# One-pass values and sums, a cap by minimum and a new weave in the second layer of a two-layer AdaLN block

## The chip, the cores and the metric

The kernel runs on one core of one Trainium2 chip. Its five engines are TensorE (PE in the profile; PEld is its weight load), VectorE (DVE), ScalarE (ACT), GpSimd (POOL) and SyncE (SP, which here only issues DMAs). The metric is the device time of one execution in microseconds (us), as a median of several runs.

## The reference, cut to what matters

Eight sequences of 256 tokens with 512 channels go through two layers. Each layer has an attention-like part and a feed-forward part; each part is normed, scaled and shifted by vectors that come from a condition, and added to the residual. Layer 0 (a selective scan and a gated feed-forward part) is not touched by the change. Layer 1 is:

```python
h = _layernorm(x) * (1 + ca) + sa
q, k, v = (proj(wq), proj(wk), proj(wv))      # 32 heads of 16 channels
q, k = _apply_rope(q, sin, cos), _apply_rope(k, sin, cos)
scores = einsum('bnth,bnsh->bnts', q, k) / sqrt(16)
scores = where(causal, scores, -inf)
attn = softmax(scores)
x = x + ga * (einsum('bnts,bnsh->bnth', attn, v) @ wo.T)
h = _layernorm(x) * (1 + cb) + sb
x1, x2 = split(h @ w12.T + b12)
x = x + gb * ((silu(x1) * x2) @ w3.T + b3)
```

## The kernel before

**Layout.** Channels lie on the 128 partitions in four groups (index j or k, `NC` = 4), tokens on the free axis. All matmuls of layer 1 are in float32, except those that write the causal mask, which are in bfloat16. A float32 matmul of the program is two instructions in the profile.

**Heads.** A group of 128 channels holds eight heads of 16. Four strips of 32 rows (r) hold two heads each, the even and the odd one (e). `ke[e]` and `qe[e]` are copies of the rotated keys and queries in which the other head's rows are blanked by `em_sb` (1 for the rows of one parity, 0 for the other). In a blanked row `ke` carries a one, and into the same row of `qe` a DMA later puts minus the row's maximum, so that the second score matmul gives score minus maximum by itself.

**The work of one batch** is written as Python generators. Each `yield` ends a step.

- `before_scores(b)`, 8 steps: mean; variance and norm (`norm_steps`, lines 72 to 95); two groups of k, two of q (line 541, each with `rotary`, line 518); two of v (line 561), copied into a padded tile `vpad` (line 566).
- `maxima(b)`, 7 steps: six tiles of scores by query (`sc`, line 588, on top of a mask matmul, line 579), each reduced to its row maximum on VectorE (line 593); in the seventh the maxima are turned by a matmul (`pnt`, line 600), copied by ScalarE (`nmt`, line 605) and sent by eight DMAs from SP's queue into rows of `qe` (line 609).
- `weigh(b)`: six tiles of scores by key (`st`, line 629), again on top of a mask matmul (line 620), each followed by one exp on ScalarE (`pt`, line 634). Key block 1 is done for two channel groups at a time, key block 0 for one. `average(j)` (line 640) multiplies the weights with the values and, in a second pass with a matrix of ones (`sumw`), with ones: `av[:, 0]` holds the sums of values, `av[:, 1]` the sums of weights. VectorE takes the reciprocal (line 655) and multiplies (line 656).
- `after_average(b)`, 10 steps: output projection `po` (2 steps, line 676), mean and variance of the second norm, four groups of the feed-forward part `pf` (line 696) with Silu on ScalarE and one multiply on VectorE, two groups of `pw` (line 710), whose result ScalarE scales (`g`, line 716) and GpSimd adds to x (line 720).

**PSUM.** The score tiles `sc` and `st` fill four banks and there is one buffer of them (`ps_sc`), so the next tile's matmuls wait until ScalarE or VectorE has read the one before. `av` has one buffer (`ps_av`), the dense groups two (`ps_mm`), the statistics one (`ps_st`).

**Order.** TensorE's order in layer 1 is written by hand: `woven` runs the 14 steps of `scores(b)` and takes, behind each, the next step of `after_average(b - 1)` (stream 0) or of `before_scores(b + 1)` (stream 1) by the list `behind` in line 738. On the other engines a scheduler sets the order when the program is built; each of them then works its queue strictly in that order. While batch b's scores are made, the output part of batch b - 1 and the q, k and v of batch b + 1 thus fill in.

Of the kernel before, what the change touches and what calls it, by code (L numbers as in the profile page):

```python
# [18 lines left out]
P = 128  # L19
# [22 lines left out]
    return ap.unsqueeze(1).to_broadcast([ap.shape[0], n, ap.shape[1]])  # L42


@with_exitstack
def block(
    ctx: ExitStack, tc: tile.TileContext,
# [21 lines left out]
    xT = [None] * NB  # L69
    mod = [[const.tile([P, NC, NB], F32, name=f"mod{l}_{v}") for v in range(6)] for l in range(2)]  # L70

    def norm_steps(lnp, ps_st, b, shift, scale1, name, put):
        xb = xT[b]
        mean = ps_st.tile([P, L], F32, name=f"mean{name}", tag="st")
        for k in range(NC):
            nc.tensor.matmul(mean, ones, xb[:, k, :], start=(k == 0), stop=(k == NC - 1))
        xc = lnp.tile([P, NC, L], F32, name=f"xc{name}", tag="xc")
        nc.vector.tensor_tensor(xc, xb, bc(mean, NC), ALU.subtract)
        h = lnp.tile([P, NC, L], F32, name=f"h{name}", tag="h")
        sq = h  # L80
        nc.scalar.activation(sq, xc, AF.Square)
        yield
        var = ps_st.tile([P, L], F32, name=f"var{name}", tag="st")
        for k in range(NC):
            nc.tensor.matmul(var, ones, sq[:, k, :], start=(k == 0), stop=(k == NC - 1))
        rstd = lnp.tile([P, L], F32, name=f"rstd{name}", tag="rstd")
        nc.scalar.activation(rstd, var, AF.Ln, bias=eps)
        nc.scalar.activation(rstd, rstd, AF.Exp, scale=-0.5)
        nc.vector.tensor_tensor(xc, xc, bc(rstd, NC), ALU.mult)  # L89
        for k in range(NC):  # L90
            nc.gpsimd.tensor_scalar(  # L91
                h[:, k, :], xc[:, k, :], scale1[:, k, b : b + 1], shift[:, k, b : b + 1],
                ALU.mult, ALU.add,
            )
        put.append(h)

    ENG = mybir.EngineType
# [380 lines left out]
    w12_sb = load(attw, w12, "w12")  # L478
    b12_sb = load(attw, b12, "b12")
    w3_sb = load(attw, w3, "w3")  # L480
    b3_sb = load(attw, b3, "b3")
    gb3 = attw.tile([P, NC, NB], F32, name="gb3")
    nc.vector.tensor_tensor(
# [2 lines left out]
    identh = attw.tile([P, P], BF16, name="identh")  # L486
    nc.vector.tensor_copy(identh, ident)

    masks = []
    for name, sign in (("qk", 1), ("kq", -1)):  # L490
        m = attw.tile([P, P], BF16, name=f"mask{name}")
        nc.gpsimd.memset(m, 0.0)
        nc.gpsimd.affine_select(
            out=m, in_=m, compare_op=ALU.is_ge, fill=MASKED,
            base=0, pattern=[[-sign, P]], channel_multiplier=sign,
        )
        masks.append(m)
    mask_qk, mask_kq = masks
    swap = [(i // HD) * HD + (i % HD + HD // 2) % HD for i in range(32)]

    strips = attw.tile([P, 2, 4], F32, name="strips")
# [5 lines left out]
    one_row = attw.tile([P, 2], F32, name="one_row")  # L507
    nc.vector.tensor_reduce(one_row, strips, AX.X, ALU.add)

    sumw = attw.tile([P, 2, 2 * HD], F32, name="sumw")  # L510
    vps = [attw.tile([P, 2, NH // 2, 4, HD], F32, name=f"vpad{i}") for i in range(2)]
    nc.gpsimd.memset(vps[0], 0.0)
    nc.gpsimd.memset(vps[1], 0.0)
    nc.gpsimd.memset(sumw, 0.0)
    for e in range(2):
        nc.gpsimd.memset(sumw[:, e, e * HD : (e + 1) * HD], 1.0)

    def rotary(ps, dst, name):
        raw = att.tile([P, 2, L], F32, name=f"raw{name}", tag="raw")
        nc.scalar.copy(raw, ps)  # L520
        sw = att.tile([P, 2, L], F32, name=f"sw{name}", tag="sw", bufs=1)
        nc.vector.stream_shuffle(sw, raw, swap)
        nc.gpsimd.tensor_tensor(raw, raw, bc(rope_sb[:, 0, :], 2), ALU.mult)  # L523
        nc.vector.tensor_tensor(sw, sw, bc(rope_sb[:, 1, :], 2), ALU.mult)
        nc.gpsimd.tensor_tensor(dst, raw, sw, ALU.add)  # L525
# [3 lines left out]
    def before_scores(b):  # L529
# [6 lines left out]
        for w, isq in ((wk_sb, False), (wq_sb, True)):  # L536
            for k0 in range(0, NC, 2):
# [10 lines left out]
                for e in range(2):  # L548
                    if isq:
                        nc.scalar.activation(qe[e][:, cols, :], rot, AF.Copy, scale=em_sb[:, e : e + 1])  # L550
                    else:
# [2 lines left out]
                            scale=em_sb[:, e : e + 1], bias=one_row[:, e : e + 1],  # L554
                        )
                yield
        vp = vps[b % 2]
        for t in range(2):
            pv = ps_mm.tile([P, NH // 2, 2, HD], F32, name=f"pv{b}_{t}", tag="mm")
# [5 lines left out]
            for e in range(2):  # L565
                nc.vector.tensor_copy(vp[:, t, :, 3 * e, :], pv[:, :, e, :])
            yield
        qs[b], ks[b] = qe, ke

    def maxima(b):  # L570
        qe, ke = qs[b], ks[b]
# [40 lines left out]
    def weigh(b):  # L612
        qe, ke, vp = qs.pop(b), ks.pop(b), vps[b % 2]
        pts = {}

        def weights(kb, js):
            Q = L - kb * P
            sc = ps_sc.tile([P, 4, len(js), 2, Q], F32, name=f"st{b}_{kb}_{js[0]}", tag="sc")
            for r in range(4):
                nc.tensor.matmul(  # L620
                    sc[:, r, :, :, :P], identh,
                    mask_kq.unsqueeze(1).unsqueeze(1).to_broadcast([P, len(js), 2, P]),
                    start=True, stop=False, skip_group_check=True,
                )
            for j in js:
                for e in range(2):
                    for r in range(4):
                        rows = slice(32 * r, 32 * r + 32)
                        nc.tensor.matmul(  # L629
                            sc[:, r, j - js[0], e, :], ke[e][rows, j, kb * P : (kb + 1) * P],  # L630
                            qe[e][rows, j, kb * P :], start=False, stop=True, skip_group_check=True,
                        )
            pt = att.tile([P, 4, len(js), 2, Q], F32, name=f"pt{b}_{kb}_{js[0]}", tag=f"pt{kb}", bufs=2 - kb)
            nc.scalar.activation(pt, sc, AF.Exp, scale=ATT_SCALE)  # L634
            for j in js:
                pts[kb, j] = pt[:, :, j - js[0]]

        ao = aos[b] = att.tile([P, NC, L], F32, name=f"ao{b}", tag="ao", bufs=1)

        def average(j):  # L640
            av = ps_av.tile([P, 2, L], F32, name=f"av{b}_{j}", tag="av")
            for kb in range(2):
                for e in range(2):
                    for what in range(2):
                        for r in range(4):
                            w = sumw[:, e, :]
                            if what == 0:
                                w = vp[:, kb, 4 * j + r, 2 * e : 2 * e + 2, :].rearrange("p a d -> p (a d)")
                            nc.tensor.matmul(  # L649
                                av[32 * r : 32 * r + 32, what, kb * P :], w, pts[kb, j][:, r, e, :],  # L650
                                start=(kb == 0 and e == 0 and what == 0), stop=(kb == 1 and e == 1),
                                skip_group_check=True,
                            )
            rec = att.tile([P, L], F32, name=f"rec{b}_{j}", tag="rec")
            nc.vector.reciprocal(rec, av[:, 1, :])  # L655
            nc.vector.tensor_tensor(ao[:, j, :], av[:, 0, :], rec, ALU.mult)

        for j in range(0, NC, 2):
            weights(1, (j, j + 1))
            yield  # L660
            weights(0, (j,))
            yield
            weights(0, (j + 1,))
            average(j)
            yield
            average(j + 1)
            if j + 2 == NC:
                yield

    def after_average(b):  # L670
        ao = aos.pop(b)
# [12 lines left out]
                )  # L684
            yield
        put = []
        yield from norm_steps(lnp, ps_st, b, mod[1][3], mod[1][4], f"d{b}", put)
        h = put[0]
        yield
        x4 = att.tile([P, NC, L], F32, name=f"x4_{b}", tag="x4", bufs=1)  # L690
        for i in range(M2 // P):
# [6 lines left out]
                        start=(k == 0), stop=(k == NC - 1),  # L698
                    )
            sl = att.tile([P, L], F32, name=f"sl{b}_{i}", tag="sl")  # L700
            nc.scalar.activation(sl, pf[:, 0, :], AF.Silu, bias=b12_sb[:, i : i + 1])  # L701
            nc.vector.scalar_tensor_tensor(  # L702
                x4[:, i, :], pf[:, 1, :], b12_sb[:, NC + i : NC + i + 1], sl, ALU.add, ALU.mult
            )
# [1 line left out]
        for k0 in range(0, NC, 2):  # L706
# [5 lines left out]
                        start=(k == 0), stop=(k == NC - 1),  # L712
                    )
            for j in (k0, k0 + 1):
                g = att.tile([P, L], F32, name=f"g{b}_{j}", tag="gout")
                nc.scalar.activation(  # L716
                    g, po[:, j - k0, :], AF.Identity,
                    bias=gb3[:, j, b : b + 1], scale=mod[1][5][:, j, b : b + 1],
                )
                nc.gpsimd.tensor_tensor(xT[b][:, j, :], xT[b][:, j, :], g, ALU.add)  # L720
            yield
        nc.sync.dma_start(out[b], xT[b])

    def woven(steps, fillers):

        fillers = [f for f in fillers if f is not None]
        for behind, _ in steps:
            for f in behind:
                if f < len(fillers):
                    next(fillers[f], None)  # L730
        for f in fillers:
            for _ in f:
                pass

    def scores(b):


        behind = [(1,), (0,), (0, 1), (0, 1), (1,), (0, 1), (1, 1), (1,), (0,), (0,), (0,), (0,), (0,), (0,)]
        i = 0
        for part in (maxima(b), weigh(b)):  # L740
            for _ in part:
                yield behind[i] if i < len(behind) else (), None
                i += 1

    with tc.manual_schedule(engines={mybir.EngineType.PE}):
        for _ in before_scores(0):
            pass
        for b in range(NB):
            last = after_average(b - 1) if b else iter(())
            ahead = before_scores(b + 1) if b + 1 < NB else iter(())  # L750
            woven(scores(b), [last, ahead])
        for _ in after_average(NB - 1):
            pass


# [81 lines left out]
```

## Time and profile before

| | us |
|---|---|
| median of 3 runs | 1714.06 (1712.4 to 1715.23) |
| the profiled execution's own time | 1717.07 |
| its span, first to last instruction | 1715.2 |
| what lies around the span | 1.9 |
| TensorE busy | 1500.7 (87%) |
| VectorE busy | 923.9 (54%) |
| ScalarE busy | 856.5 (50%) |
| GpSimd busy | 739.0 (43%) |
| mean granted TensorE clock | 0.933 of full speed |

The span is counted from the first instruction to the last. Layer 1's own norm begins near 866 us, and its first score tile at 907.40 us. A "start of a batch" below is the start of the first mask matmul of its first score tile (line 579). Busy time counts an engine's computing instructions only; "PEclk" is the TensorE clock that was granted, in tenths or hundredths of full speed. In a timeline a row gives start, length, engine, line, operation, result and inputs, the number of merged instructions, and in square brackets the idle time of the engine just before and what ended it.

### The profile page before, as it was taken

How to read it: one execution, taken by the hardware profiler on the slowest of the kernel's cores; microseconds unless marked ns; L12 is line 12 of the kernel's file. 1: busy time of each engine (PE TensorE's matmuls, PEld its weight loads, DVE VectorE, ACT ScalarE, POOL GpSimd, SP SyncE). 2: the span in 40 equal slices, each digit the busy share in tenths (PEclk: the TensorE clock that was granted, in tenths of full speed). 3: DMA queues.
4: the chain of work that ended last, by engine and by line, in shares of the span. 5: the costliest groups of instructions: out<-in, count | busy, mean ns of one | idle time of the engine just before them, and what ended most of it. 6: DMA issues, size and time to landing. Idle time of an engine off the chain costs nothing. (4 is left out here: it accounts for less than half of the span.)

```text
span 1715.2 us, 23134 instructions
## 1 busy us (share of the span) xinstructions
PE 1500.7 (87%) x9632; PEld 1159.8 (68%) x9632; DVE 923.9 (54%) x865; ACT 856.5 (50%) x1290; POOL 739.0 (43%) x570
## 2 busy tenths in 40 slices
PE   5298889898989898988978799989999899989797
PEld 4277677777777777866855475757677576757575
DVE  0378798989898989871115252433425243342421
ACT  2363777777787877642022325344353534435152
POOL 0287788888888888980122111130302113030001
PEclk9565799999999999989989899999999999999898
DMA  1945422222222232220220000000000000000000
GB/s 66 357 167 186 167 81 93 98 100 98 100 98 99 99 100 97 100 74 0 79 100 0 2 1 2 13 2 13 2 2 13 2 13 2 14 2 2 14 13 13
DMA packets 31273, 106.43 MB, mean 62 GB/s; under 512 B 4657, under 2 KB 5297, under 8 KB 30017
## 3 DMA queue, kind: packets, MB, share of 16 engines
q1 hardware_dynamic: 29440, 93.28, 15.8%
q10 hardware_dynamic: 1728, 11.68, 1.7%
q8 instruction: 75, 1.23, 0.3%
q14 instruction: 30, 0.24, 0.0%
HBM read 100.23 MB, written 4.46 MB: 61 GB/s over the span
## 5 line engine op out<-in xcount | busy, mean ns | idle before, releaser
L287 POOL TENSOR_TENSOR hs<-hs,bc 128x1024 f32<-128x1024 f32 x128 | 302.5, 2363 | 156.5 <-DVE hs L283 142.8
L283 DVE TENSOR_TENSOR_SCAN hs<-dA,bx 128x1024 f32<-128x1024 f32 x128 | 292.0, 2281 | 26.7 <-ACT dA L269 19.6
L269 ACT ACTIVATE dA<-dt,alog 128x255 f32<-128x255 f32 x512 | 216.6, 495 | 132.8 <-DVE hs L283 106.3
L338 PE MATMUL pg<-hb,wg 128*128 128x256 f32 (+1 forms) x704 | 167.5, 391 | 19.9 <-ACT sg L346 18.3
L338 PE MATMUL pu<-hb,wu 128*128 128x256 f32 (+1 forms) x704 | 167.9, 392 | 18.7 <-DVE mid L351 18.7
L288 POOL TENSOR_TENSOR hs<-hs 128x512 f32<-128x512 f32 x128 | 177.0, 1383 | 10.0
L360 PE MATMUL down<-mid,wd 128*128 128x256 f32 (+1 forms) x704 | 159.0, 382 | 12.6 <-DVE x L365 11.8
L338 PEld LDWEIGHTS pg<-hb,wg 128*128 128x128 f32 (+1 forms) x704 | 132.8, 192 | 50.0 <-ACT sg L346 25.7
L338 PEld LDWEIGHTS pu<-hb,wu 128*128 128x128 f32 (+1 forms) x704 | 135.2, 194 | 46.3 <-DVE mid L351 23.7
L720 POOL TENSOR_TENSOR x<-x,g 128x256 f32<-128x256 f32 x32 | 22.7, 730 | 333.5 <-ACT g L716 333.5
L278 DVE TENSOR_TENSOR bx<-ub,bc 128x1024 f32<-128x1024 f32 x128 | 157.3, 1229 | 6.2 <-DMA bc<-bcd 3.5
L360 PEld LDWEIGHTS down<-mid,wd 128*128 128x128 f32 (+1 forms) x704 | 132.4, 190 | 36.8 <-DVE x L365 19.5
L593 DVE TENSOR_REDUCE nm<-sc 128x8 f32<-128x1024 f32 (+1 forms) x64 | 110.9, 1754 | 42.0 <-PE sc L588 42.0
L696 PE MATMUL pf<-hd,w 128*128 128x256 f32 x512 | 124.2, 398 | 4.3 <-POOL hd L91 4.3
L696 PEld LDWEIGHTS pf<-hd,w 128*128 128x128 f32 x512 | 99.2, 198 | 26.2 <-issue 7.0
L655 DVE RECIPROCAL rec<-av 128x256 f32<-128x256 f32 x32 | 56.2, 1758 | 112.2 <-PE av L649 112.2
L634 ACT ACTIVATE pt<-st 128x2048 f32<-128x2048 f32 x48 | 89.9, 1874 | 40.0 <-PE st L629 39.7
L290 POOL TENSOR_TENSOR ys<-hs 128x256 f32<-128x256 f32 x128 | 100.7, 787 | 10.0
L702 DVE SCALAR_TENSOR_TENSOR x<-pf,b,sl 128x256 f32<-128x256 f32 x32 | 15.5, 484 | 158.2 <-ACT sl L701 158.2
L91 POOL TENSOR_SCALAR hc<-xcc,mod,mod 128x256 f32<-128x256 f32 x32 | 17.3, 554 | 193.1 <-DVE xcc L89 193.1
L306 PE MATMUL y<-ys,ident 128*128 128x256 f32 x256 | 86.3, 423 | 7.5 <-POOL ys L290 7.4
L129 PEld LDWEIGHTS mps<-c,wm 128*128 128x128 f32 x384 | 75.8, 297 | 24.8 <-issue 10.1
(150 smaller groups left out, 2498.8 us busy)
## 6 DMA issues: line engine op xcount, KB each, us to landing
bc<-bcd SPq DMA_DIRECT2D x128, 512.0 KB
wm<-in_wmod_dram SPq DMA_DIRECT2D x12, 1024.0 KB
out_dram<-x SPq DMA_DIRECT2D x8, 512.0 KB
x<-in_x_dram ACTq DMA_DIRECT2D x6, 512.0 KB
wd<-in_wd_dram ACTq DMA_DIRECT2D x1, 2816.0 KB
wg<-in_wg_dram ACTq DMA_DIRECT2D x1, 2752.0 KB
wu<-in_wu_dram ACTq DMA_DIRECT2D x1, 2752.0 KB
w<-in_w_dram SPq DMA_DIRECT2D x1, 2048.0 KB
```

The source lines that it names most:

```text
L269: nc.scalar.activation(da[:, n, 1:], dts[b][:, k, 1:], AF.Exp, scale=a_sb[:, k, i : i + 1])
L278: nc.vector.tensor_tensor(bx, bc(ubs[b, pair][:, kk, :], NQ), bcs[b, pair, q][:, 0], ALU.mult)
L283: nc.vector.tensor_tensor_scan(hs.rearrange("p n l -> p (n l)"), das.pop((b, s)).rearrange("p n l -> p (n l)"), hss.pop((b, s)).rearrange( ...
L287: nc.gpsimd.tensor_tensor(hs, hs, bcs[b, pair, q][:, 1], ALU.mult)
L288: nc.gpsimd.tensor_tensor(hs[:, 0:2, :], hs[:, 0:2, :], hs[:, 2:4, :], ALU.add)
L290: nc.gpsimd.tensor_tensor(ys, hs[:, 0, :], hs[:, 1, :], ALU.add)
L306: nc.tensor.matmul(ypair[b, pair][:, kk, :], ident, ysum.pop((b, s)), start=False, stop=(q == NS // NQ - 1), skip_group_check=True,)
L338: nc.tensor.matmul(ps[:m, i - i0, :], w[:, k, i * P : i * P + m], h[:, k, :], start=(k == 0), stop=(k == NC - 1),)
L360: nc.tensor.matmul(pd, wd_sb[:m, i, k * P : (k + 1) * P], mid[:m, i, :], start=(i == 0), stop=(i == NI - 1),)
L593: nc.vector.tensor_reduce(nm[:, qb, :, j, :].rearrange("p e r -> p r e"), sc[:, :, j - j0, :, :], AX.X, ALU.max, negate=True,)
L634: nc.scalar.activation(pt, sc, AF.Exp, scale=ATT_SCALE)
L696: nc.tensor.matmul(pf[:, g, :], w12_sb[:, k, m0 : m0 + P], h[:, k, :], start=(k == 0), stop=(k == NC - 1),)
```

## The change

All of it is in layer 1.

- **Cap.** The mask matmuls under the `st` tiles go. Instead VectorE takes, in place in PSUM, the minimum of the diagonal part of the tile with a tile `cap_kq` that holds +1e30 where a key is allowed and -1e30 where it isn't. The exp then waits for that minimum. (The `sc` tiles keep their mask matmul.)
- **One pass.** The padding of `vpad` is one instead of zero. One matmul per head then gives values in its own 16 rows and sums of weights in the other head's 16 rows, for even and odd heads in separate columns (`av[:, e]`). ScalarE keeps the odd rows (`odd`), VectorE blends the rest in by two operations, takes the reciprocal, swaps the 16-row halves (a shuffle) and multiplies. `sumw` goes.
- **Silu from tanh.** Silu becomes (tanh(y/2) + 1) * (y/2): two activations on ScalarE and one more operation on VectorE for each group.
- **Norm.** Mean and variance share one PSUM tile; in `after_average` the last scale and shift are done by ScalarE instead of GpSimd.
- **Buffers.** `raw`, `rec` and `gout` have one buffer instead of two.
- **Weave.** `scores` has 17 steps, since both averages of each half now end in a yield. There are three streams: BEHIND (output part of b - 1), AHEAD (q, k, v of b + 1) and LATER (mean and variance of b + 2). Each step but two has at least one of them behind it; the steps 3, 5 and 7 have two.

```diff
+        qs[b], ks[b] = qe, ke
...
         def weights(kb, js):
-            for r in range(4):
-                nc.tensor.matmul(sc[:, r, :, :, :P], identh, mask_kq..., start=True, stop=False)
...
-                            qe[e][rows, j, kb * P :], start=False, stop=True, skip_group_check=True,
+                            qe[e][rows, j, kb * P :], start=(j == js[0] and e == 0), stop=True,
+            own = sc.rearrange("p r j e q -> p (r j e) q")[:, :, :P]
+            nc.vector.tensor_tensor(own, own, bc(cap_kq, 8 * len(js)), ALU.min)
...
         def average(j):
-                    for what in range(2):
...
-            nc.vector.reciprocal(rec, av[:, 1, :])
-            nc.vector.tensor_tensor(ao[:, j, :], av[:, 0, :], rec, ALU.mult)
+            nc.scalar.activation(odd, av, AF.Copy, scale=em_sb[:, 1:2])
+            nc.vector.scalar_tensor_tensor(rec, av[:, 1, :], em_sb[:, 0:1], odd[:, 0, :], ALU.mult, ALU.add)
+            nc.vector.scalar_tensor_tensor(ao[:, j, :], av[:, 0, :], em_sb[:, 0:1], odd[:, 1, :], ALU.mult, ALU.add)
+            nc.vector.reciprocal(rec, rec)
+            nc.vector.stream_shuffle(div, rec, [(i + HD) % 32 for i in range(32)])
+            nc.vector.tensor_tensor(ao[:, j, :], ao[:, j, :], div, ALU.mult)
...
             weights(0, (j + 1,))
+            yield
             average(j)
             yield
             average(j + 1)
-            if j + 2 == NC:
-                yield
+            yield
...
-            nc.scalar.activation(sl, pf[:, 0, :], AF.Silu, bias=b12_sb[:, i : i + 1])
+            nc.scalar.activation(sl, pf[:, 0, :], AF.Tanh, bias=hb12[:, i : i + 1], scale=0.5)
+            nc.scalar.activation(half, pf[:, 0, :], AF.Identity, bias=hb12[:, i : i + 1], scale=0.5)
+            nc.vector.scalar_tensor_tensor(sl, sl, 1.0, half, ALU.add, ALU.mult)
...
-        behind = [(1,), (0,), (0, 1), (0, 1), (1,), (0, 1), (1, 1), (1,), (0,), (0,), (0,), (0,), (0,), (0,)]
+    BEHIND, AHEAD, LATER = range(3)
+    turns = [
+        (AHEAD,), (BEHIND,), (BEHIND,), (AHEAD, BEHIND), (AHEAD,), (AHEAD, BEHIND), (AHEAD,),
+        (AHEAD, LATER), (BEHIND,), (BEHIND,), (LATER,), (), (BEHIND,), (BEHIND,), (), (BEHIND,), (BEHIND,),
+    ]
     with tc.manual_schedule(engines={mybir.EngineType.PE}):
+        ahead, later = before_scores(0), before_scores(1)
+        turn(ahead, 2 + NC + 2)
+        turn(later, 2)
+        behind = None
+        for b in range(NB):
+            ahead, later = later, before_scores(b + 2) if b + 2 < NB else None
+            for after in zip_turns(scores(b), turns):
+                for which in after:
+                    turn((behind, ahead, later)[which])
```

The scheduler's order on the other engines moves with it. In the changed program ScalarE's queue for batches 2 to 6 reads, around the maxima: raw (second q group), table load, Ln of the second norm, the two copies into q, table load, Exp, **nmt**, four scalings of the second norm, exp of the first `st` tile. For batches 0, 1 and 7 nmt stands ahead of the Exp and of those copies into q. VectorE's queue around the second `st` pair reads: blends, reciprocal, shuffle and product of average 0, first blend of average 1, norm product (batches 0 to 5), second blend, reciprocal of average 1, **minimum of the pair**.

## The prediction

> **What bounds the kernel now.** First the busy time by stretches of the span, cut at each batch's first score tile. The columns are stretch and length, then busy time and (count) of PE, PEld, DVE, ACT, POOL, then granted clock, DMA share, GB/s.
>
> ```profile
> 907.40:990.56 83.16, 64.27 (x661) 42.44 (x659) 30.43 (x34) 24.95 (x26) 14.75 (x13) 0.92 0.01 1
> 990.56:1088.80 98.24, 92.51 (x808) 66.64 (x805) 39.89 (x46) 41.31 (x43) 17.89 (x18) 0.98 0.01 1
> 1088.80:1188.58 99.78, 92.45 (x805) 67.12 (x804) 37.84 (x44) 42.32 (x45) 19.26 (x20) 0.98 0.02 7
> ...
> 1484.76:1585.00 100.24, 94.22 (x806) 67.65 (x805) 37.81 (x44) 42.32 (x45) 19.28 (x20) 0.97 0.02 7
> 1585.00:1667.94 82.94, 71.08 (x709) 52.13 (x708) 28.65 (x26) 30.22 (x28) 4.99 (x8) 0.92 0.02 8
> ```
>
> A middle batch takes 98.2 to 99.8 us (batches 2 to 5: mean 99.0) and PE is busy 92.5 of it; no other engine passes 43. PE is the bound, with some 7 us of holes. Next the timeline, for the holes of batch 2:
>
> ```profile
> 1130.60 0.36 ACT L605 COPY nmt<-pnt 32x256 f32<-32x256 f32 x1
> ...
> 1130.98 4.53 SPq L609 DMA_DIRECT2D q<-nmt  x8
> ...
> 1136.94 1.33 ACT L550 ACTIVATE q<-rot_True,emask 128x512 f32<-128x512 f32 x2 [5.98 <-POOL rot_True L525]
> 1138.17 0.56 ACT L520 COPY raw_True<-pqk_True 128x512 f32<-128x512 f32 x1
> 1138.79 3.70 PE L561 MATMUL pv<-wv,hc 128*128 128x512 f32 x8 [2.37 <-ACT raw_True L520]
> ...
> 1142.82 1.33 ACT L550 ACTIVATE q<-rot_True,emask 128x512 f32<-128x512 f32 x2 [4.08 <-POOL rot_True L525]
> ...
> 1145.96 0.60 PE L620 MATMUL st<-maskkq,identh 128*128 128x256 bf16 x4 [3.47 <-ACT pt L634]
> 1146.49 1.27 PE L629 MATMUL st<-q,k 32*128 32x256 f32 x16
> 1147.69 5.24 PE L696 MATMUL pf<-hd,w 128*128 128x256 f32 x16
> ```
>
> The holes come from ScalarE's strict queue: a copy waits behind q, which waits for the rotary on GpSimd; then PE waits for the copy, and later for the exp. And after the 3.47 us hole the pf group takes 5.24 where others take 3.72: a clock penalty of about 1.6. Last, batch 7, where nothing hides the DMAs that carry the maxima:
>
> ```profile
> 1617.53 0.34 ACT L605 COPY nmt<-pnt 32x256 f32<-32x256 f32 x1
> ...
> 1619.57 0.50 PE L629 MATMUL st<-q,k 32*128 32x128 f32 x8 [2.67 <-DMA q<-nmt]
> ...
> 1621.89 1.67 PE L629 MATMUL st<-q,k 32*128 32x128 f32 x24 [1.81 <-DMA q<-nmt]
> ```
>
> nmt ends at 1617.87; the even rows are there 1.7 later, the odd ones (the fifth of eight DMAs) 4.0 later.
>
> **What leaves PE.** From start to start at full clock (timeline of batch 2), `st` with mask takes 2.07 (pair) or 1.60, without it 1.10 or 1.07: 2 x 0.97 + 4 x 0.53 = 4.1 us. An average takes 2.74, half of it with `sumw`: 4 x 1.37 = 5.5. Together 9.5 per batch, 76 in eight. The whole batch at full clock: scores 2 x 2.06 + 4 x 1.60, k and q 4 x 3.56, v 2 x 3.53, eight output groups x 3.56, statistics 4 x 1.73, pnt 0.56, `st` 10.5, averages 11.0 = 89.3. So before loses 99.0 - 89.3 = 9.7, and after has 79.8 of work. The question is what after loses.
>
> **What is added elsewhere.** VectorE per batch: minima 2 x 2.3 + 4 x 1.22 (the bx row, 128x1024 with a PSUM source, has 1.23; the reduce of 2048 has 2.29), four averages each 3.5 (two blends at 0.48 as in line 702, reciprocal 1.76, shuffle 0.4 and product 0.4 by halving the 512 rows of 0.73 and 0.69) for 2.2, four times 0.4 for silu: 37.8 + 9.5 + 5.3 + 1.6 = 54. ScalarE: eight table loads of 1.28 go (Silu and the exp after it; the changed order holds 4 loads per batch for 12), four `odd` at 0.66, four `half` at 0.5 and 2.3 of norm come: 42.3 - 10.3 + 6.9 = 39. GpSimd loses 2.2. Neither sum bounds a batch of 80; the chains through their queues do.
>
> **Stall A, the maxima.** I walk batch 2 with PE at full clock from 0: steps 0 to 5 have no wait (each reduce, 2.3, lies under a dense group of 3.56), q's second group ends at 33.6, pnt at 35.9, the first v group at 39.4. ScalarE: k's second raw copy 21.6, the k pair at 26.25 to 27.8 (a rotary takes 4.65 from raw to its result: 1138.17 to 1142.82), square to 28.9, raw of q's first group, its q pair 33.6 to 34.9, raw of the second, Ln under its rotary, q pair 39.6 to 40.9, table load and Exp to 42.7, nmt to 43.05. So the rows arrive at 44.75 and 47.05, and the `st` pair ends at 48.7 where 40.5 was possible: 8.2 lost, and 1.6 of clock behind it. Before, a q group and a v group hid this; now a v group alone does. In batch 1 nmt stands ahead of the Exp and q pair, at 37.4: 1.8 lost, no clock.
>
> **Stall B, the cap.** Between `st` tiles lies now minimum + exp: 2.3 + 1.9 for a pair, 1.2 + 1.9 for a single. The v group with LATER's mean (5.3), and pf0 and pf1 (3.56 each, exp wait 3.2 and the two silu operations) hide the first three. Not so the pair of step 12. With 0 at the end of average 0's matmuls: `odd` waits for half and ends at 0.95, blends 2.25, average 1 starts (0.65 lost behind 1.73 of variance) and ends at 3.6; VectorE works off reciprocal, shuffle, product, first blend, then waits for the Exp (6.1), norm product 7.35, blend, reciprocal to 9.65, and only then the minimum, to 12.0; exp to 13.95. PE had the pair done at 4.7 and pf2 at 8.4: 5.7 lost, 1.6 of clock. Before average 3 another 0.9, since it waits for exp, `odd` and blends. Together 8.9.
>
> **Sum.** Batches 2 to 5: 79.8 + 9.8 + 8.9 = 98.5 for 99.0, -0.5 each, -2. Batch 1: 90.5 for 98.24, -7.7. Batch 6 has no LATER (less 1.73 of mean, and no norm product in stall B, 1.8): 95.0 for 100.24, -5.3. Batch 0 has the same statistics but bare `st` steps: waits of 3.4, 1.8, about 9, 3.2 and 3.5; with the mean and variance of batch 1 now ahead of it I come to its end at 993 for 990.56, +2.5. Batch 7: 80.5 for 82.94, -2.4. Tail: longer silu before the last pw (0.6), one `gout` buffer (0.6), last blends: +1.5. Sum -13.5 on the profiled 1717.07. That run is 3.0 above the median, so I forecast 1714.06 - 13.5 = **1700.5**.
>
> **Bounds of what is not shown.** The in-place minimum of a pair: from 1.88 (the exp of 2048) to twice the 2.3 taken; each 0.1 of it costs about 0.4 per batch; I take 2.3 by the bx row, the nearest kind. Tanh from 0.42 (Exp row) to 0.56 (g row): under 0.2 on a path; I take Silu's 0.47. Reciprocal from SBUF: 1.6 to 1.8, same row. `odd` 0.57 to 0.8 by the raw and k rows. One buffer of raw costs nothing: its next copy already stands behind k or q in ScalarE's queue. Moving the norm's scaling to ScalarE costs nothing while stall A lasts; without it the four scalings (2.3) would stand before the exp.
>
> **The skill.** After a hole of 2.40 the next v group took 5.40 in batch 3 and 3.70 in batch 4; after 3.47, 5.24. The Trainium skill, "TensorE: Matmul & The Clock Gate", section "HAM oscillation", says that PE gaps over about 3.4 us bring back the half clock. That speaks against this change, which trades shorter holes for two of 5 us a batch; an estimate by that page makes each cost up to 1.7, close to my 1.6 from the row. The trace shows loads of 1.28 with the next activation 0.02 behind. "ScalarE: Activation LUTs", section "What ACT_TABLE_LOAD costs", adds a drain, 2.66 in all; by it ScalarE would save 21 us a batch and not 10, still off the path.
>
> **Rivals.**
> *The stalls are hidden.* For: ScalarE's and VectorE's sums are half a batch, and if nmt came as early as in batch 1, stall A would fall by 8 in five batches: 1700 - 40 = 1660. Against: the queue orders above. At best, losses as before: 1714 - 76 = 1638.
> *Slower by the minimum in PSUM.* If reading and writing the same bank in place takes twice the bx row, the pair costs 2.3 more in stall B, singles 1.2 each where cover is 3.56: some 6 per batch, 1700 + 48 = 1748. It decides from 1.7 per batch, a minimum 20% or so longer. Against: bx itself reads and writes PSUM.
> *No change*, the losses 1.5 per batch above my walk: 1712.
> *The change doesn't do what it says* (tanh needs its own table) is excluded by the four loads per batch.
>
> **Chances.** Forecast, small gain (1685 to 1710.5): 0.50. Hidden, under 1685: 0.15. Within 0.2% (3.4 us, about what a measurement can tell from no change): 0.12. Slower: 0.23, half of it over 1727. Range 1658 to 1732, which leaves out some 0.1 above and 0.05 below.
>
> **What would show it.** Right: PE waits of 5 us for the q<-nmt DMAs in batches 2 to 6 but not in batch 1; about 5.7 us before the first `st` single of the second half, released by its exp; batch periods near 98 and 90 (batch 1). Wrong: a `st` minimum far from 2.3 and 1.2; nmt before 40 in the batch; PE busy over 85% of a middle batch.

## The result and the profile after

The change made the kernel slightly slower: 1721.91 us (median of 17 runs, 1714.7 to 1727.04) beside 1715.05 us (17 runs, 1711.18 to 1720.85) for the kernel before; ratio 1.0036, 95% interval 1.0021 to 1.005. The forecast was 1700.5, a gain of 13.5; measured is a loss of 6.9.

The profiled execution of the changed kernel took 1718.43 us with a span of 1716.6, at a mean clock of 0.908 (before 0.933). The two spans differ by only 1.4 because layer 0, which the change doesn't touch, happened to end 4.0 us earlier in this execution (over all runs below, layer 1's first variance starts between 866.1 and 872.8 us). So all that follows is counted in layer 1, from its first variance to the end of the span: 842.95 us before, 848.3 after, +5.35. TensorE's busy time fell from 1500.7 to 1453.9, and VectorE's rose from 923.9 to 1051.1.

These are the changed kernel's busy times by stretches cut at the same places as before the change: stretch and length, busy time and (count) of PE, PEld, DVE, ACT, POOL, then granted clock, DMA share, GB/s.

```profile
911.19:1000.40 89.21, 62.53 (x509) 39.63 (x508) 43.94 (x51) 27.75 (x30) 16.62 (x16) 0.77 0.00 1
1000.40:1092.44 92.04, 85.18 (x657) 62.84 (x654) 56.23 (x73) 37.78 (x48) 15.77 (x14) 0.95 0.00 1
1092.44:1190.89 98.45, 86.59 (x654) 63.83 (x653) 53.78 (x71) 38.34 (x49) 17.22 (x16) 0.93 0.02 7
1487.77:1583.09 95.32, 83.43 (x637) 61.13 (x636) 51.32 (x69) 33.82 (x44) 15.07 (x12) 0.93 0.02 7
1583.09:1668.92 85.83, 66.82 (x557) 49.45 (x556) 44.28 (x53) 26.17 (x32) 2.92 (x4) 0.84 0.02 8
```

The rows are batches 0, 1, 2, 6 and 7. TensorE has some 150 matmul instructions less in a middle batch and yet batch 2 takes 98.45 us, where it took 99.78 before. The clock column tells where to look: batch 0 ran at 0.77 (0.92 before), batch 7 at 0.84 (0.92), a middle batch at 0.93 (0.98).

Next the timeline around the maxima in batch 2: start, duration, engine, line, operation, and in brackets the idle time before it and who ended it.

```profile
1127.87 0.63 PE L607 MATMUL pnt<-ident,nm 128*32 128x128 f32 x4
...
1129.01 0.47 ACT L93 ACTIVATE rstdd<-statsd,eps 128x256 f32<-128x256 f32 x1
...
1131.78 1.33 ACT L557 ACTIVATE q<-rot_True,emask 128x512 f32<-128x512 f32 x2 [2.30 <-POOL rot_True L532]
1133.13 1.28 ACT L94 ACT_TABLE_LOAD   x1
1134.42 0.42 ACT L94 ACTIVATE rstdd<-rstdd 128x256 f32<-128x256 f32 x1
1134.75 0.34 ACT L612 COPY nmt<-pnt 32x256 f32<-32x256 f32 x1
...
1136.88 0.81 PE L630 MATMUL st<-q,k 32*128 32x128 f32 x8 [4.76 <-DMA q<-nmt]
1139.12 1.67 PE L630 MATMUL st<-q,k 32*128 32x128 f32 x24 [1.42 <-DMA q<-nmt]
1140.71 5.00 PE L569 MATMUL pv<-wv,hc 128*128 128x512 f32 x8
```

`pnt` is done at 1128.5 and the copy `nmt` starts only at 1134.75, behind q's second pair, a table load and the Exp. TensorE waits 4.76 and 1.42 for the DMAs that follow, and the v group behind the waits takes 5.00 instead of 3.70. ("Half clock" below means that matmuls take twice their usual time, as the `st` of 2.09 for 1.15 in the next view; a longer group such as this one is slow only at its start.) This is stall A of the prediction. Stall B is 30 us later, in the same view:

```profile
1164.26 1.23 DVE L95 TENSOR_TENSOR xcc<-xcc,rstdc 128x1024 f32<-128x1024 f32 x1 [1.24 <-ACT rstdc L94]
1165.40 0.48 DVE L660 SCALAR_TENSOR_TENSOR ao<-av,emask,odd 128x256 f32<-128x256 f32 x1
...
1165.79 1.74 DVE L663 RECIPROCAL rec<-rec 128x256 f32<-128x256 f32 x1
1167.45 2.27 DVE L636 TENSOR_TENSOR st<-st,capkq 128x2048 f32<-128x2048 f32 x1
...
1169.76 1.88 ACT L638 ACTIVATE pt<-st 128x2048 f32<-128x2048 f32 x1 [5.54 <-DVE st L636]
...
1171.69 2.09 PE L630 MATMUL st<-q,k 32*128 32x256 f32 x16 [5.24 <-ACT pt L638]
...
1173.71 5.57 PE L706 MATMUL pf<-hd,w 128*128 128x256 f32 x16
```

The pair's `st` was ready at 1162.8; its minimum starts at 1167.45, behind norm product, blend and reciprocal. The `st` and `pf` behind the wait run at half clock (2.09 for 1.15, 5.57 for 3.72). Batch 2 thus loses 4.76 + 1.42 + 5.24 + 0.44 = 11.9 in waits and 5.0 by the clock.

By stretches (batch starts as defined above; the tail begins with the last `po`):

| | before | after | forecast | measured |
|---|---|---|---|---|
| prologue (first variance to first score tile) | 35.15 | 42.89 | | +7.7 |
| prologue and batch 0 | 118.31 | 132.10 | +2.5 | +13.8 |
| batch 1 | 98.24 | 92.04 | -7.7 | -6.2 |
| batches 2 to 5 together | 395.96 | 395.33 | -2.0 | -0.6 |
| batch 6 | 100.24 | 95.32 | -5.3 | -4.9 |
| batch 7 | 82.94 | 85.83 | -2.4 | +2.9 |
| tail | 47.26 | 47.68 | +1.5 | +0.4 |

The middle came out as forecast. The two ends did not: 11.3 and 5.3 us over the forecast. In the prologue and batch 0 the timeline of TensorE reads:

```profile
907.71 3.68 PE L91 MATMUL statsc<-hc,ones 128*128 128x256 f32 x8 [2.40 <-ACT hc L88]
...
955.41 5.40 PE L569 MATMUL pv<-wv,hc 128*128 128x512 f32 x8
...
966.94 2.09 PE L630 MATMUL st<-q,k 32*128 32x256 f32 x16 [3.33 <-ACT pt L638]
968.96 2.79 PE L650 MATMUL av<-pt,vpad 128*32 128x256 f32 x32
...
985.26 2.09 PE L630 MATMUL st<-q,k 32*128 32x256 f32 x16 [8.56 <-ACT pt L638]
990.68 2.09 PE L630 MATMUL st<-q,k 32*128 32x256 f32 x16 [3.33 <-ACT pt L638]
```

The waits are those forecast (3.33, 8.56 and 3.33 for 3.4, about 9 and 3.2), but what stands behind them takes nearly twice its time (averages 2.79 for 1.51).

### The profile page after: what moved, and what is told of

It is laid out like the page before. It is cut to its first block, busy times and chain, and to the rows that moved or that the text cites. A ratio compares the mean times of both kernels' runs of the same rounds, so it can differ in the third digit from the quotient of the medians.

```text
span 1716.6 us, 20951 instructions
## 1 busy us (share of the span) xinstructions
PE 1453.9 (85%) x8416; PEld 1132.9 (66%) x8416; DVE 1051.1 (61%) x1074; ACT 833.6 (49%) x1329; POOL 722.4 (42%) x535
## 5 line engine op out<-in xcount | busy, mean ns | idle before, releaser
L630 PE MATMUL st<-q,k 32*128 32x256 f32 (+1 forms) x1024 | 72.5, 413 | 91.4 <-ACT pt L638 52.3
L706 PE MATMUL pf<-hd,w 128*128 128x256 f32 x512 | 134.6, 423 | 4.2 <-ACT hd L99 4.2
L706 PEld LDWEIGHTS pf<-hd,w 128*128 128x128 f32 x512 | 106.6, 213 | 30.9 <-issue 9.2
L630 PEld LDWEIGHTS st<-q,k 32*128 32x128 f32 x1024 | 48.9, 226 | 114.6 <-ACT pt L638 58.7
L636 DVE TENSOR_TENSOR st<-st,capkq 128x1024 f32<-128x1024 f32 (+1 forms) x48 | 75.9, 1582 | 46.8 <-PE st L630 46.8
L530 POOL TENSOR_TENSOR raw_False<-raw_False,rope 128x512 f32<-128x512 f32 x16 | 28.4, 1772 | 155.7 <-DVE sw_False L529 155.7
```

The costliest lines, as they stand in the source:

```text
L630: nc.tensor.matmul(sc[:, r, j - js[0], e, :], ke[e][rows, j, kb * P : (kb + 1) * P], qe[e][rows, j, kb * P :], start=(j == js[0] and e == ...
L636: nc.vector.tensor_tensor(own, own, bc(cap_kq, 8 * len(js)), ALU.min)
L706: nc.tensor.matmul(pf[:, g, :], w12_sb[:, k, m0 : m0 + P], h[:, k, :], start=(k == 0), stop=(k == NC - 1),)
```

## The experiments

The theory: the matmul time that the change takes from TensorE is given back at three places, the late maxima (A), the late minimum of the pair (B), and half clock behind waits, above all in the thin batches 0 and 7. The rivals: the minimum in PSUM or the blends cost by their own duration; the new order costs by itself; one chain stands behind both waits. Every time is a median, beside 1715 to 1718 us for the kernel before on the same chip; "period" is that of a middle batch (mean of 2 to 5), 99.0 before and 98.8 after; "layer 1" is counted as above.

**e1: the maxima by another queue.**

```diff
-        nc.scalar.copy(nmt, pnt)
+        nc.vector.tensor_copy(nmt, pnt)
```

> The changed kernel with one line altered: the copy nmt, which carries the maxima from PSUM to SBUF ahead of their eight DMAs, is made by VectorE and not by ScalarE. Theory (the matmul time that the change saved is given back by three things: the maxima that come late through ScalarE's queue, the pair's minimum that comes late through VectorE's queue, and half clock in batches 0 and 7): in batches 2 to 6 nmt ends some 4.5 to 5.5 us earlier, the two waits for q<-nmt (4.8 and 1.4 us in batch 2) shrink to under 1.5 together, and the v group behind them runs at full clock; 4 to 7 us per batch, 20 to 35 in all, so 1687 to 1702. Rival one (the minimum in PSUM and the blends of the single pass are what costs): under 10 us in all, since what follows the maxima sets the pace. Rival two (the order of 17 steps itself costs): no change.

1679.73 us, ratio to before 0.9785 (0.9766 to 0.9804); period 92.2. From its timeline in batch 2:

```profile
1124.03 0.62 PE L607 MATMUL pnt<-ident,nm 128*32 128x128 f32 x4
...
1125.36 0.40 DVE L612 COPY nmt<-pnt 32x256 f32<-32x256 f32 x1
...
1128.22 0.50 PE L630 MATMUL st<-q,k 32*128 32x128 f32 x8
...
1129.84 1.05 PE L630 MATMUL st<-q,k 32*128 32x128 f32 x24 [1.12 <-DMA q<-nmt]
...
1130.82 3.70 PE L569 MATMUL pv<-wv,hc 128*128 128x512 f32 x8
```

The copy starts 0.7 us behind the end of `pnt` instead of 6.2. The waits fall from 6.18 to 1.12 (0.85 appear at the next `st`), the v group is back at 3.70. Stall A is worth 6.6 a batch: one line turns the change into a gain of some 2%, more than expected, since batches 0 and 7 gained 4.3 and 3.5 us too.

**e3: the cap undone** (mask matmuls back, no minimum).

```diff
+            for r in range(4):
+                nc.tensor.matmul(sc[:, r, :, :, :P], identh, mask_kq..., start=True, stop=False)
...
-            own = sc.rearrange("p r j e q -> p (r j e) q")[:, :, :P]
-            nc.vector.tensor_tensor(own, own, bc(cap_kq, 8 * len(js)), ALU.min)
```

> The changed kernel with the cap undone: the four mask matmuls per score tile in front of st are back and the minimum is gone; all else as changed. Theory: TensorE gets back 4.1 us of work per batch, but the wait for the pair's exp behind reciprocal and norm product on VectorE (5.2 us) goes, with its clock penalty, and the thin batch 0 keeps TensorE busier; some 3 to 5 us less per middle batch, 5 to 10 less in batch 0: 1680 to 1700. Rival one (the blends and the single pass cost, not the minimum): 4 us more per batch, 1750. Rival two (the order of steps): within 10 us of the changed kernel.

1670.55 us (0.9728, 0.9705 to 0.9752); period 92.9, and 3.83 and 1.52 of wait for the maxima are all that is left in it. Batch 0 fell from 89.2 to 78.9. So 4 us more of matmuls per batch took 6 off the period: more than expected. As the last edit added, the cap cost 51 us (1721.91 - 1670.55). The first rival had expected 1750, so the blends and the single pass are not what costs.

**e4: the single pass undone** (second pass with `sumw`, reciprocal and product from PSUM).

```diff
+                    for what in range(2):
...
-            nc.scalar.activation(odd, av, AF.Copy, scale=em_sb[:, 1:2])
...
+            nc.vector.reciprocal(rec, av[:, 1, :])
+            nc.vector.tensor_tensor(ao[:, j, :], av[:, 0, :], rec, ALU.mult)
```

> The changed kernel with the single pass undone: the sums come from a second set of matmuls with sumw, then reciprocal and product straight from PSUM, as before the change; cap, silu and steps stay as changed. Theory: TensorE gets 5.5 us more per batch, and the shorter chain on VectorE (odd, two blends and shuffle go, about 2.2 us per average) gives back 2 to 3 of it: 1735 to 1750. Rival (the blends and odd, on the way from average to average, are what eats the gain): no slower than the changed kernel, 1700 to 1720.

1723.99 us (1.0036, 1.0015 to 1.0058): within the scatter of the changed kernel's 1721.91, between what the theory and the rival had expected and nearer to the rival. TensorE has 5.5 us more of work in a batch and the period is 98.0. From its timeline in the batch that starts at 1190.15:

```profile
1264.68 3.72 PE L704 MATMUL pf<-hd,w 128*128 128x256 f32 x16
1270.12 1.15 PE L634 MATMUL st<-q,k 32*128 32x256 f32 x16 [1.73 <-ACT pt L642]
1271.20 3.72 PE L704 MATMUL pf<-hd,w 128*128 128x256 f32 x16
```

The wait before the `st` is 1.73 instead of 5.24, and the clock stays whole behind it (1.15 and 3.72): 3.5 + 0.9 + 1.9 gained, 0.4 more at the next average, 5.5 spent. So under the cap the single pass buys nothing: what it saves on TensorE goes into a longer stall B.

**e5: the second pair ahead of the second average.**

```diff
             average(j)
             yield
+            if j + 2 < NC:
+                weights(1, (j + 2, j + 3))
+                yield
             average(j + 1)
```

> The changed kernel with one step moved: the st matmuls, minimum and exp of the second pair stand ahead of the second average and not behind it, so that the minimum is no longer queued on VectorE behind the second average's blends and reciprocal. Theory: the pair's minimum starts some 1.5 to 3 us earlier (it still stands behind the norm product in a middle batch, not in batches 0, 6 and 7), and the wait of 5.2 us ahead of the next st shrinks by that, with its clock penalty where it falls under 3; 2 to 5 us per batch, 1690 to 1708. Rival (the minimum's own duration in PSUM is the loss, wherever it stands): within 4 us of the changed kernel.

1672.54 us (0.975, 0.9728 to 0.9772); period 92.3, batch 0 80.0 for 89.2. From its timeline in batch 2:

```profile
1149.32 1.23 DVE L95 TENSOR_TENSOR xcc<-xcc,rstdc 128x1024 f32<-128x1024 f32 x1
...
1150.46 2.29 DVE L636 TENSOR_TENSOR st<-st,capkq 128x2048 f32<-128x2048 f32 x1
...
1152.79 1.88 ACT L638 ACTIVATE pt<-st 128x2048 f32<-128x2048 f32 x1 [2.55 <-DVE st L636]
...
1154.72 1.15 PE L630 MATMUL st<-q,k 32*128 32x256 f32 x16 [1.58 <-ACT pt L638]
```

The minimum takes the same 2.29 as ever and now starts 2.4 us behind its `st` instead of 4.7. That shortens the wait from 5.24 to 1.58 (0.64 appear at the next `st`) and keeps the clock whole. The minimum's own duration is excluded as the cause: its place in the queue was. The gain was more than expected: in a middle batch some 3.3 us of wait and 2.8 of clock, and 9.2 in batch 0.

**e10: matmuls that nobody reads, in the waits of batches 0 and 7.**

```diff
+    def warm(b, i):
+        n = {0: {1: 8, 2: 8, 8: 12, 12: 32, 13: 12}, NB - 1: {0: 8, 7: 16, 12: 10}}.get(b, {}).get(i, 0)
...
+            for _ in range(n):
+                nc.tensor.matmul(ps, identh, mask_qk.unsqueeze(1).to_broadcast([P, 4, P]), start=True, stop=True)
```

> The changed kernel with matmuls added whose result nobody reads (128x512 in bf16, in groups of 8 to 32) in the waits of batch 0 (five places) and batch 7 (three places); nothing else is altered. Theory (half clock after the waits is what put these two batches above the forecast): the granted clock in batch 0 rises from 0.77 to above 0.9, the averages there take 1.5 and not 2.8, the single st 1.15 and not 2.09, and in batch 7 the two pf groups of 5.4 take 3.7: 6 to 14 us less in all, 1704 to 1712 beside 1718. Rival (the waits themselves, whatever the clock): no gain, or up to 5 us more, since the added matmuls stand in TensorE's queue ahead of useful ones.

1705.16 us (0.9943, 0.9923 to 0.9963): 17 us below the changed kernel by added work alone. Batch 0 takes 81.37 for 89.21, batch 7 with the tail 126.76 for 133.51; the middle is as it was (98.9 to 99.1). First the stretches of batch 0 and of batch 7 up to its last `po`, then TensorE's timeline in batch 0:

```profile
910.77:992.14 81.37, 67.78 (x581) 40.86 (x579) 43.00 (x48) 27.74 (x30) 16.61 (x16) 0.98 0.01 1
1575.74:1654.73 78.99, 68.52 (x591) 48.28 (x590) 44.29 (x53) 26.13 (x32) 2.92 (x4) 0.94 0.02 8
```

```profile
959.39 2.77 PE L742 MATMUL warm<-maskqk,identh 128*128 128x512 bf16 x12
962.79 1.15 PE L630 MATMUL st<-q,k 32*128 32x256 f32 x16 [0.64 <-ACT pt L638]
963.87 1.51 PE L650 MATMUL av<-pt,vpad 128*32 128x256 f32 x32
...
971.39 7.08 PE L742 MATMUL warm<-maskqk,identh 128*128 128x512 bf16 x32
980.17 1.15 PE L630 MATMUL st<-q,k 32*128 32x256 f32 x16 [1.69 <-ACT pt L638]
```

The clock of batch 0 goes from 0.77 to 0.98, its `st` from 2.09 to 1.15, its averages from 2.79 to 1.51. The chain over minimum and exp takes what it took (9.73 us from the start of the pair's `st` to the next `st` in the changed kernel, 9.88 here); only the matmuls behind the waits are faster. So it is the clock that put these batches above the forecast. (The waits for the maxima in batch 7, 2.21 and 1.42, and a v group of 5.40 in batch 0 are left.)

**e2: the edit of e1 in the kernel before** (control).

> The kernel before the change, with nmt copied by VectorE and not by ScalarE and nothing else altered. Theory (the late maxima became a wait only by the change, since before a q group and a v group hid them in the middle batches): 0 to 3 us less in all, all of it in batch 7 where nothing hid them: 1712 to 1716. Rival (the copy on ScalarE is a loss in any order of steps): 4 us or more per middle batch, under 1690.

1714.88 us, no change (ratio 1.001, 0.9994 to 1.0025). Before the change the copy on ScalarE cost nothing: stall A is a wait that the change made.

**e9: the old operations in the new order of 17 steps.**

> The kernel before the change with only the order of its steps altered, to the 17 steps of the changed kernel; mask matmuls, second pass and silu stay as before. Theory: the order alone brings the late maxima (about 5.3 of waits and some 3 of clock per middle batch) and takes away the waits that the old order had (some 5 to 7 per batch with their clock): close to 98 us per middle batch and 1705 to 1722 in all; so the change in order is worth nothing by itself, and the matmuls saved came on top of it. Rival one (the new order is itself a loss): over 1735. Rival two (the new order is itself the gain): under 1695.

1677.38 us (0.9783, 0.9764 to 0.9802), as rival two had it: the new order by itself was a gain of 38 us. Stretches of a middle batch:

```profile
1084.62:1175.66 91.04, 90.18 (x805) 66.86 (x804) 38.08 (x44) 41.04 (x44) 19.31 (x20) 1.00 0.02 7
```

The clock is whole and TensorE is busy 90.18 of 91.04. The theory was wrong in one point here: the late maxima do not come with the order of steps. In this kernel's queue `nmt` stands ahead of the Exp and of q's second pair, and the wait for it is 0.35.

**e13: silu put back, all else as changed.** So which edit moved `nmt` back in ScalarE's queue? In the traces, `nmt` stands behind the Exp and q's second pair in batch 2 of every kernel that has the tanh form, the copy on ScalarE and the new order (the changed one, e3, e4, e5 and e10), so also with the cap or the single pass undone.

```diff
-            nc.scalar.activation(sl, pf[:, 0, :], AF.Tanh, ...)
-            nc.scalar.activation(half, pf[:, 0, :], AF.Identity, ...)
-            nc.vector.scalar_tensor_tensor(sl, sl, 1.0, half, ALU.add, ALU.mult)
+            nc.scalar.activation(sl, pf[:, 0, :], AF.Silu, bias=b12_sb[:, i : i + 1])
```

> The changed kernel with only silu put back to the Silu activation (tanh, half and the extra VectorE operation go). On ScalarE's queue the copy nmt then stands ahead of the Exp and of q's second pair, where the changed kernel has it behind them. Theory (the late maxima are a matter of queue order, and it is the silu edit, not the order of steps, that set it): nmt ends some 5 us earlier, the waits for q<-nmt nearly go, while the table loads come back on an engine that has room; 4 to 6 us less per middle batch, the wait of 5.2 us ahead of the st single stays, 1680 to 1700. Rival (the 8 table loads per batch, 1.28 us each, that tanh removed were a gain on the path): slower than the changed kernel, 1730 or more.

1681.21 us (0.9785, 0.9759 to 0.9811); period 90.6. From its timeline in a middle batch:

```profile
1135.43 0.47 ACT L93 ACTIVATE rstdd<-statsd,eps 128x256 f32<-128x256 f32 x1
...
1135.80 0.34 ACT L612 COPY nmt<-pnt 32x256 f32<-32x256 f32 x1
1136.17 1.28 ACT L94 ACT_TABLE_LOAD   x1
...
1138.20 1.33 ACT L557 ACTIVATE q<-rot_True,emask 128x512 f32<-128x512 f32 x2 [0.33 <-POOL rot_True L532]
```

`nmt` follows the Ln at once, and the wait for the maxima is 1.23. Stall B is as before (5.06). The table loads that tanh saves are worth nothing here: with them back the kernel is 41 us faster. Of the 8.2 us that a middle batch gains, 6.6 are what e1 gained, so most of what tanh did to the time was done by the order in which the scheduler then queued ScalarE's work. Where the other 1.6 come from is not shown by a run of its own; two short waits that e1 still has (0.85 at the `st` behind the first minimum, 0.45 at the last average) are absent here. The edits of norm and buffers were not undone one by one.

**e8: the new operations in the old order of 14 steps.**

> The changed kernel with the old order of 14 steps; single pass, minimum and silu from tanh stay. Theory: the new order by itself was a gain of 38 us (the kernel before with the new order: 1677), and the old order has longer waits for the minimum, since it puts no dense group behind most st steps; 20 to 50 us slower than the changed kernel, 1740 to 1770. Rival (the new order pays only with the old operations, and with the new ones both orders end at the same waits): 1710 to 1735.

1726.49 us (1.0054, 1.0037 to 1.0072), as the rival had it. With e9 it makes a square. Layer 1 in us:

| | old order | new order |
|---|---|---|
| old operations | 842.95 (before) | 807.42 (e9) |
| new operations | 851.54 (e8) | 848.30 (after) |

The order is worth 35.5 with the old operations and 3.2 with the new ones; the new operations, with less matmul work, cost 8.6 in the old order and 40.9 in the new.

**e12: the edits of e1 and e3 together. e6: those of e1 and e5 together.**

> The changed kernel with the mask matmuls back in place of the minimum, and nmt copied by VectorE: both edits that helped alone (92.3 and 92.15 us per middle batch beside 98.9). Theory (two separate waits, each with its own clock penalty): the edits add up, since the one takes the wait for the maxima away and the other the wait for the pair's exp; 92.3 - 6.7, near 86 us per middle batch, against 83.9 of matmul work at full clock (79.8 + 4.1), 1632 to 1645 in all. Rival (one chain behind both waits, so that taking one away leaves nothing for the other): within 10 us of either alone, 1662 to 1672.

> The changed kernel with the copy nmt on VectorE and the second pair's st, minimum and exp ahead of the second average: the two edits that gave 6.7 and 6.6 us per middle batch alone. Theory (two separate waits): they add up to 85.6 us per middle batch against 79.8 of matmul work at full clock, 1625 to 1640. Rival (one chain behind both): within 10 us of either alone, 1662 to 1682.

e12: 1626.24 us (0.9486, 0.9471 to 0.9501), period 85.3. e6: 1642.24 us (0.9562, 0.9541 to 0.9582), period 86.1. e12 is 6 us below what was expected, e6 2 above. In both kernels the two edits add up in the middle batches (86.3 and 85.7 by subtraction), so A and B are separate waits and no chain stands behind both. A middle batch of each, e12 first:

```profile
1161.66:1246.95 85.29, 85.04 (x677) 62.80 (x676) 44.77 (x66) 37.87 (x48) 17.64 (x16) 1.00 0.02 8
```

```profile
1168.04:1254.08 86.04, 81.66 (x654) 60.67 (x653) 54.10 (x72) 37.90 (x48) 17.53 (x16) 1.00 0.02 8
```

In e12 TensorE is busy for all but 0.25 us of the batch: nothing but matmul work is left. e6 has 3.4 us less of busy time and 4.4 us of short waits, 3.1 of them behind the minimum and 1.1 for the maxima, so it stays the slower one; it also lost more at the ends (81.8 for 74.7 in batch 0).

**e14: e12 with unread matmuls in the waits that were left** (prologue, batch 0, batch 7, tail).

> The changed kernel with the mask matmuls back, nmt on VectorE (1626 without more), and groups of 6 to 16 matmuls that nobody reads in the remaining waits of the prologue, of batch 0, of batch 7 and of the tail behind it. Theory (half clock behind waits of over 2 us is the rest of the loss there): the prologue's second statistic takes 1.9 and not 3.7, batch 0 falls by 3 to 5 us, batch 7 with the tail by 4 to 6, 1612 to 1620. Rival (those stretches are set by chains on the other engines, and TensorE's clock is of no account): 1624 or more.

1622.58 us (0.9449, 0.9426 to 0.9473), 3.7 below e12 and some 2.6 short of what was expected. Batch 0 gained 3.2 and batch 7 with the tail 1.3. The prologue gained nothing: its second statistic ran at 1.99 instead of 3.68, but now its second v group took 5.40 for 3.70, where in e12 the first one had. It is the fastest version, 5.5% under the kernel before.

## Why the prediction was wrong

**TensorE's saving** of 9.5 a batch was nearly right: TensorE's busy time at full clock is 90.18 in e9, 85.04 in e12 (5.1 less, by the second pass) and 81.66 in e6 (3.4 less, by the masks), 8.5 in all. From period to period the second pass shows as 5.75 (91.04 in e9, 85.29 in e12; 5.5 taken).

**Added work** was priced right. The minimum took 2.29 and 1.23 (2.3 and 1.22 taken), which ends the rival of a dearer minimum: the kernel did become slower, but not by that. Blends took 0.47, reciprocal 1.74, shuffle 0.44, product 0.42, `odd` 0.69, tanh and half 0.47 each; there was no table load for tanh. In batch 2 VectorE was busy 53.78 and ScalarE 38.34, for sums of 54 and 39.

**Stall A** was right in place and cause: waits of 6.2 and 2.2 of clock (8.2 and 1.6 forecast) in batches 2 to 6, and a wait of 1.18 in batch 1. **Stall B** likewise: 5.24 and 0.44 of wait and 2.8 of clock, 8.5 for 8.9. (The prediction writes 5.7 for the first wait where its own times give 13.95 - 8.4 = 5.55.) The two are 1.8 less than forecast, and the matmul work is as much more: e6 is busy 81.66 at full clock, where the sum of rows gave 79.8. Half of that is in the base (e9, the old operations, 90.18 for 89.3) and half in the saving. So the middle periods of 98.45 to 99.08, for the 98.5 forecast, are right partly by luck, because two errors cancel; batch 1, with 92.04 for 90.5, shows the larger matmul work. One sign of error that the prediction named did appear, TensorE busy over 85% of a middle batch (86.59 of 98.45), and it was badly chosen: matmuls at half clock count as busy. e6, without those, has 81.66, and 5.0 of clock make up the difference.

**The step that failed** is the sum over the thin stretches, in which TensorE works in short bursts between waits: "Batch 0 has the same statistics but bare `st` steps: waits of 3.4, 1.8, about 9, 3.2 and 3.5 ... I come to its end at 993 for 990.56, +2.5", and "Batch 7: 80.5 for 82.94". In batch 0 the waits were right (the two ahead of averages, 1.8 and 3.5, are 1.55 and 3.47 in e10, where the clock is nearly whole) and the clock was left out behind them, though the prediction had put 1.6 behind each long wait of a middle batch; for batch 7 it lists no waits, so only the total can be compared. Prologue and batch 0 cost 13.8, batch 7 2.9 more than before. e10 took 14.6 us off these two ends (7.8 and 6.8) by restoring the clock. What it did not reach in prologue and batch 0 are two groups at half clock, the prologue's second statistic (3.68 for 1.99) and a v group (5.40 for 3.70), 1.7 each by the rows. With the 7.8 that batch 0 gained that is 11.2 of the 11.3 by which the two stood over the forecast. The last 3.4 are counted, not shown: in e14 the statistic came back to 1.99 and the prologue gained nothing.

**The hidden-stalls rival** (1660) had the mechanism of what was possible: an earlier `nmt` (e1) gives 1680, with the cap undone as well 1626. The prediction took the compiled queue order as given, and the traces show the stalls where that order puts them. It costed tanh at nothing on the path; e13 shows that by queue order it was, of the three operations undone alone, the dearest next to the cap (1681.21 and 1670.55 without them, 1723.99 without the single pass, for 1721.91).

**The clock.** Waits of 2.4 us were enough to lose it: in the changed kernel a statistic took 3.68 for 1.99 behind a wait of 2.40, and the score tiles of batch 0 took 2.02 and 2.09 for 1.15 behind waits of 2.56 and 2.39. The prediction had such a row in hand, a v group of 5.40 for 3.70 behind a hole of 2.40 in a middle batch of the kernel before, and counted clock only behind the long waits. The Trainium skill, "TensorE: Matmul & The Clock Gate", section "HAM oscillation", speaks of gaps over about 3.4 us. The rows decide: a wait of 2.4 us can cost the clock too. The same page's section "What's actually happening" has the clock set by a free-running window of activity, which does not reset when a kernel starts. The unequal answers to equal waits below fit that; no run here shows the window itself.

## What to carry to other kernels

Time taken off the bounding engine pays only as far as no strict queue behind it has a late instruction: walk each queue's compiled order for the one short instruction that a DMA or the next matmul waits for, and move that first; here one copy and one pair's minimum were worth some 6.5 us a batch each. Price the clock behind waits of 2.4 us as well, not only behind the long ones, above all where little dense work stands between the waits: batch 0 lost most by it here. When several edits come together, time them in a square (each with and without the other), since two that look like savings can hide or undo a third's gain.

## What the runs showed that was not expected

- Matmuls that nobody reads, put into waits, made the kernel faster by 17 us (e10), since there the half-clock stretches cost more than they do.
- The answer to a short wait is not a matter of its length alone. In batch 7 of e12 a wait of 2.41 us was followed by a mask group at half clock (1.01 for 0.60); in e14, at the same place, the wait was 2.41 and the group took 0.60.
- Undoing an edit that had freed the busiest engine (e3: 4 us more of matmuls per batch) gave the largest gain of any single edit, 51 us.
